# Edge masks of a graph layer made on GpSimd between adjacency products, with a new order of the pair loop

## The chip, the cores and the metric

The kernel runs on one core of a Trainium2 chip. The metric is the device time of one execution in microseconds (us); each figure below is the median of several executions, with the lowest and highest beside it where that matters. The engines are called by the names in the profile: PE (TensorE), PEld (its weight loads), DVE (VectorE), ACT (ScalarE), POOL (GpSimd), SP (SyncE, which issues transfers).

## The reference, cut to what matters

There are 3327 nodes with 64 features and a dense adjacency of fp32 zeros and ones. Layer 0 is a hyperbolic graph layer: for every pair of nodes it needs an attention weight and the logarithmic map of one node at the other, and sums over the neighbours. Layer 1 weights each node's last 100 neighbours by powers of one half, according to their rank from the right.

```python
# layer 0
adj_att = sigmoid(left[:, None] + right[None, :] + b_att[0]) * adj
x_local = logmap(x[:, None, :], x[None, :, :], c)
support_t = einsum('ij,ijd->id', adj_att, x_local)
out0 = proj(expmap(x, support_t, c), c)
# layer 1
mask = (adj != 0).astype(support.dtype)
rank = jnp.cumsum(mask, axis=1)
deg = rank[:, -1:]
k = jnp.minimum(deg, 100.0)
pos = rank - (deg - k)
w = mask * jnp.where(pos > 0, 0.5 ** (k - pos), 0.0)
out1 = w @ support + bias
```

What matters is what the adjacency is read for. Layer 0 multiplies it, as fp32, into the sigmoid. Layer 1 needs a bf16 mask of it, so that PE can count with triangular matrices how many neighbours lie to the right.

## The kernel before

The adjacency is cut into four strips of columns (8, 8, 6 and 4 blocks of 128) and each strip into rounds of at most 1024 columns' worth. A round loads a tile `ad`, makes the mask, lets PE add to the counts in PSUM (`pc`), reads the counts out as uint8 (on ACT or on DVE), builds the sigmoid (a tanh, then the *adjacency product*), computes the pair products in PSUM (`pq`), puts two gelus over them, multiplies with the sigmoid (the *final product*), and lets PE sum (the *total*, in `po`).

```python
for b0, nb in STRIPS:
    ...                                   # loads and left factors of the strip
    for hi in range(NB, 0, -per):
        ad = work.tile([P, FMAX], F32, name="ad", bufs=4)
        nc.sync.dma_start(ad..., adj_t[lo * P : hi * P, i0 : i0 + F]...)
        mask = work.tile([P, FMAX], BF16, name="mask", bufs=3)
        V.tensor_scalar(mask[:, :span], ad[:, :span], 0.0, None, op0=ALU.not_equal)
        for j in js:
            ...                           # counts: matmuls with ca (block before) and cb (this block)
            if j % (2 if b0 == 0 else 4):
                A.activation(kept, pc[:, :F], AF.Relu)
            else:
                V.tensor_scalar(kept, pc[:, :F], 0.0, None, op0=ALU.max)
        sg = work.tile([P, FMAX], F32, name="sg", bufs=3)
        for j in js:
            A.activation(part(sg, j), left_b[:, :F], AF.Tanh, bias=right[:, j : j + 1], scale=0.5)
        V.scalar_tensor_tensor(sg[:, :span], sg[:, :span], 1.0, ad[:, :span], op0=ALU.add, op1=ALU.mult)
        pq = ps.tile([P, FMAX], F32, name="pq", bufs=2)
        ...                               # two matmuls per half and block
        s = work.tile([P, FMAX], F32, name="s", bufs=3)
        A.activation(s[:, :span], pq[:, :span], AF.Gelu, scale=-WG / QS)
        A.activation(s[:, :span], s[:, :span], AF.Gelu, scale=WH)
        V.scalar_tensor_tensor(s[:, :span], s[:, :span], WD, sg[:, :span], op0=ALU.add, op1=ALU.mult)
        ...                               # total of this round into po
        next(steps, None)                 # one step of the post-processing of the strip before
```

The sums of a finished strip are post-processed during the next one, by many short DVE instructions on 128x8 numbers (norms, reciprocal square roots) and some on 128x512, slipped in between the rounds.

Of the kernel before, what the change touches and what calls it, by code (L numbers as in the profile page):

```python
# [11 lines left out]
F32 = mybir.dt.float32  # L12
F16 = mybir.dt.float16
BF16 = mybir.dt.bfloat16
# [3 lines left out]
AF = mybir.ActivationFunctionType  # L18
# [4 lines left out]
P = 128  # L23
# [3 lines left out]
D = 64  # L27
K = D + 2
STRIPS = [(0, 8), (8, 8), (16, 6), (22, 4)]
FMAX = 8 * P  # L30
JH = 13

GSTRIPS = [(0, 7), (7, 7), (14, 6), (20, 6)]
GFMAX = 7 * P
# [30 lines left out]


HS = 1024.0
CNT = 127.0


def halves(n):
    return [(a, min(a + 512, n)) for a in range(0, n, 512)]
# [363 lines left out]
def fast(ctx, tc, x, adj_t, r, w_att, b_att, weight, bias, out, flag):  # L436
# [27 lines left out]
    def column(value, name):  # L464
# [13 lines left out]
    G.memset(ca, -1.0)  # L478
    G.affine_select(out=cb, in_=ca, compare_op=ALU.is_gt, fill=0.0, base=0,
                    pattern=[[-1, P]], channel_multiplier=1)  # L480
    G.affine_select(out=cb, in_=cb, compare_op=ALU.not_equal, fill=CNT, base=0,
                    pattern=[[-1, P]], channel_multiplier=1)
    G.tensor_sub(ca, ca, cb)
    row1 = const.tile([1, P], BF16, name="row1")
    G.memset(row1, 1.0)
    rowc = const.tile([1, 512], BF16, name="rowc")
    G.memset(rowc, MAX_NEIGH - CNT)

    node = const.tile([P, NB], F32, name="node")
    G.memset(node, 1.0)  # L490
# [34 lines left out]
    behind_hi = const.tile([P, NB - JH, NP], U8, name="behind_hi")  # L525
    s2 = const.tile([P, NB, 2, D], F16, name="s2")

    post_pool = ctx.enter_context(tc.tile_pool(name="post", bufs=1))
    pairs = ctx.enter_context(ExitStack())
    ps = pairs.enter_context(tc.tile_pool(name="ps", bufs=1, space=PSUM))  # L530

    with tc.tile_pool(name="pre", bufs=1) as pre:
# [102 lines left out]
        V.tensor_mul(right, plr[:, :, 1], yr)  # L635
        V.tensor_scalar(right, right, batt, 0.5, op0=ALU.add, op1=ALU.mult)


        wn, opx = small("wn"), small("opx")
        V.tensor_scalar(wn, nrm, WA / 2, None, op0=ALU.mult)  # L640
# [16 lines left out]
    def behind(j):  # L657
        return behind_lo[:, j] if j < JH else behind_hi[:, j - JH]

    def in_range():  # L660

        st = post_pool.tile([P, 4], F32, name="st")
        t1 = post_pool.tile([P, NB], F32, name="st1")
        V.tensor_mul(t1, nrm, node)
        V.tensor_reduce(st[:, 0:1], t1, AX.X, ALU.max)
        V.scalar_tensor_tensor(t1, x2, c_c, t1, op0=ALU.mult, op1=ALU.mult)
        V.tensor_reduce(st[:, 1:2], t1, AX.X, ALU.max)
        V.tensor_mul(t1, bal, node)
        V.tensor_reduce(st[:, 2:3], t1, AX.X, ALU.max)
        V.tensor_reduce(st[:, 3:4], t1, AX.X, ALU.min)  # L670
        V.tensor_scalar(st[:, 3:4], st[:, 3:4], -1.0, None, op0=ALU.mult)
        pf = ps.tile([P, P], F32, name="pq", bufs=2)
        T.transpose(pf[:4, :], st, ident)
        st2 = post_pool.tile([4, 1], F32, name="st2")
        V.tensor_reduce(st2, pf[:4, :], AX.X, ALU.max)
        pf = ps.tile([P, P], F32, name="pq", bufs=2)
        T.transpose(pf[:1, :4], st2, ident[:4, :4])
        st3 = post_pool.tile([1, 4], F32, name="st3")
        V.tensor_copy(st3, pf[:1, :4])
        ok = post_pool.tile([1, 2], F32, name="ok")  # L680

        V.tensor_mul(ok, st3[:, 0:4:2], st3[:, 1:4:2])
        V.tensor_scalar(ok[:, 0:1], ok[:, 0:1], QMAX / 2, None, op0=ALU.is_le)
        V.tensor_scalar(ok[:, 1:2], ok[:, 1:2], 0.0, None, op0=ALU.is_equal)
        V.tensor_mul(ok[:, 0:1], ok[:, 0:1], ok[:, 1:2])
        V.tensor_scalar(flag, ok[:, 0:1], -1.0, 1.0, op0=ALU.mult, op1=ALU.add)
# [95 lines left out]
        V.tensor_sub(s2[:, bs, 1], w, s2[:, bs, 0])  # L782


    steps = iter(())
    for b0, nb in STRIPS:
        F = nb * P
        i0 = b0 * P
        hv = halves(F)
        blocks = slice(b0, b0 + nb)  # L790
        queue = nc.scalar if b0 == 0 else nc.sync

        iz = strip.tile([P, 8, P], F16, name="iz")[:, :nb]
        iu = strip.tile([KB, 8, P], F16, name="iu")[:, :nb]
        queue.dma_start(iu[:D], ju[:D, blocks])
        queue.dma_start(iu[D:], ju[KB : KB + 7, blocks])
        queue.dma_start(iz[:D], jz[D:, blocks])
        queue.dma_start(iz[D:], jz[:D, blocks])
        izf, iuf = iz.rearrange("p b q -> p (b q)"), iu.rearrange("p b q -> p (b q)")
        pc = ps.tile([P, FMAX], F32, name="pc")  # L800
        po = ps.tile([P, FMAX], F32, name="po")
        pl = ps.tile([P, FMAX], F32, name="pq", bufs=2)
        for b in range(nb):
            T.transpose(pl[:, b * P : (b + 1) * P], left[:, b0 + b : b0 + b + 1].to_broadcast([P, P]), ident)
        left_b = strip.tile([P, FMAX], F32, name="left_b", bufs=1)
        A.copy(left_b[:, :F], pl[:, :F])
        for f0, f1 in hv:
            T.matmul(pc[:, f0:f1], row1, rowc[:, : f1 - f0], start=True, stop=True, skip_group_check=True)

        per = FMAX // F  # L810
        before = None
        for hi in range(NB, 0, -per):
            lo = max(hi - per, 0)
            js = range(hi - 1, lo - 1, -1)
            span = (hi - lo) * F

            def part(t, j, a=0, b=F):
                return t[:, (j - lo) * F + a : (j - lo) * F + b]

            ad = work.tile([P, FMAX], F32, name="ad", bufs=4)  # L820
            nc.sync.dma_start(ad[:, :span].rearrange("p (b f) -> p b f", f=F),
                              adj_t[lo * P : hi * P, i0 : i0 + F].rearrange("(b p) f -> p b f", p=P))
            mask = work.tile([P, FMAX], BF16, name="mask", bufs=3)
            V.tensor_scalar(mask[:, :span], ad[:, :span], 0.0, None, op0=ALU.not_equal)  # L824
            for j in js:
                now = part(mask, j)
                for f0, f1 in hv:
                    if before is not None:
                        T.matmul(pc[:, f0:f1], ca, before[:, f0:f1], start=False, stop=True, skip_group_check=True)  # L829
                    T.matmul(pc[:, f0:f1], cb, now[:, f0:f1], start=False, stop=True, skip_group_check=True)  # L830
                before = now
                kept = behind(j)[:, i0 : i0 + F]
                if j % (2 if b0 == 0 else 4):
                    A.activation(kept, pc[:, :F], AF.Relu)  # L834
                else:
                    V.tensor_scalar(kept, pc[:, :F], 0.0, None, op0=ALU.max)  # L836


            sg = work.tile([P, FMAX], F32, name="sg", bufs=3)
            for j in js:  # L840
                A.activation(part(sg, j), left_b[:, :F], AF.Tanh, bias=right[:, j : j + 1], scale=0.5)  # L841
            V.scalar_tensor_tensor(sg[:, :span], sg[:, :span], 1.0, ad[:, :span], op0=ALU.add, op1=ALU.mult)  # L842

            pq = ps.tile([P, FMAX], F32, name="pq", bufs=2)
            for j in js:
                for f0, f1 in hv:
                    T.matmul(part(pq, j, f0, f1), ju[:KB, j, :], iuf[:, f0:f1], start=True, stop=False)  # L847
                    T.matmul(part(pq, j, f0, f1), jz[:, j, :], izf[:, f0:f1], start=False, stop=True)  # L848
            s = work.tile([P, FMAX], F32, name="s", bufs=3)
            A.activation(s[:, :span], pq[:, :span], AF.Gelu, scale=-WG / QS)  # L850
            A.activation(s[:, :span], s[:, :span], AF.Gelu, scale=WH)  # L851
            V.scalar_tensor_tensor(s[:, :span], s[:, :span], WD, sg[:, :span], op0=ALU.add, op1=ALU.mult)  # L852
            for j in js:
                for f0, f1 in hv:
                    T.matmul(po[: D + 1, f0:f1], hw[:, j, :], part(s, j, f0, f1), start=j == NB - 1, stop=j == 0)  # L855
                next(steps, None)
        for _ in steps:
            pass

        ot = work.tile([P, FMAX], F32, name="s", bufs=3)[: D + 1]  # L860
        V.tensor_copy(ot[:, :F], po[: D + 1, :F])
        pa = ps.tile([P, FMAX], F32, name="pq", bufs=2)
        for b in range(nb):
            c0 = (b // 4) * 512 + (b % 4) * (D + 1)
            T.transpose(pa[:, c0 : c0 + D + 1], ot[:, b * P : (b + 1) * P], ident[: D + 1, : D + 1])
        agg = post_pool.tile([P, 8, D + 1], F32, name="agg", bufs=2)
        for c in range(0, nb, 4):
            n = min(4, nb - c)
            A.copy(agg[:, c : c + n], pa[:, c * P : c * P + n * (D + 1)].rearrange("p (b d) -> p b d", b=n))
        steps = post(agg[:, :nb], b0, nb)  # L870
        if b0 == 0:
            in_range()
    pairs.close()


# [4 lines left out]
    with tc.tile_pool(name="l1", bufs=2) as l1, tc.tile_pool(name="l1_ps", bufs=1, space=PSUM) as l1_ps:  # L880
# [16 lines left out]
        for j in range(late):  # L897
            wt = decode(j)
            for n in range(len(chunks)):
                add(j, wt, n)  # L900
            for _ in range(2):
                next(steps, None)
        for _ in steps:
            pass
        weights = [decode(j) for j in range(late, NB)]
# [70 lines left out]
```

## Time and profile before

| | before |
|---|---|
| time, us (3 executions) | 460.64 (459.14 to 461.43) |
| profiled span, us | 459.1 |
| pair loop, us (first adjacency product at 47.9 to the last strip's copy at 390.3) | 342.3 |
| DVE busy, us | 407.1 |
| POOL busy, us | 13.3 |

The profile is read in three steps: which engine has no room left, in which stretch of the time, and which instructions fill it. The prediction shows those three views. A group line gives the source line, engine, operation, output and inputs by name and shape, the count, then the busy time and the mean of one in ns, then the idle time just before them and what ended most of it.

### The profile page before, as it was taken

Reading aid. Unit: us, or ns where it says so; the run is one execution under the profiler, and the core shown is the slowest. Engines: PE = TensorE matmul, PEld = TensorE weight load, DVE = VectorE, ACT = ScalarE, POOL = GpSimd, SP = SyncE. Lnnn points to the kernel's source line nnn. Section 1 sums busy time; section 2 is a strip of 40 time slices with the busy share of each in tenths; the row PEclk is TensorE's granted clock in tenths of the full one; section 3 lists DMA queues with packets and bytes.
Section 4 is the critical chain, followed back from the end, with each engine's and each line's share of the span. In section 5 each row is a group of like instructions: output and inputs, shape, how many; then the busy total and the mean of one; then the engine's idle time right before and its main releaser. Section 6 shows DMA issues by size and latency. Waiting matters only on the chain.

```text
span 459.1 us, 4660 instructions
## 1 busy us (share of the span) xinstructions
PE 378.4 (82%) x1484; PEld 153.4 (33%) x1484; DVE 407.1 (89%) x774; ACT 369.2 (80%) x423; POOL 13.3 (3%) x30
## 2 busy tenths in 40 slices
PE   0266699999989799999997999889778897699293
PEld 0035233333323233333333444434322332244152
DVE  3895689999988999999998999999999998999821
ACT  1445989999894999999995999999599995888310
POOL 6000000000000000001000000020000000000000
PEclk9997699999999999999999999999999998899877
DMA  7103354545541444444442444344533420000003
GB/s 201 62 1 72 105 168 143 141 151 163 167 135 46 133 143 140 137 137 137 137 127 75 136 137 140 106 128 125 168 93 111 121 89 1 1 1 1 0 0 82
DMA packets 22840, 47.77 MB, mean 104 GB/s; under 512 B 8652, under 2 KB 9082, under 8 KB 22808
## 3 DMA queue, kind: packets, MB, share of 16 engines
q1 hardware_dynamic: 20522, 46.47, 34.7%
q10 hardware_dynamic: 2062, 0.87, 0.9%
q0 software_dynamic: 224, 0.07, 0.3%
q8 instruction: 13, 0.21, 0.2%
q14 instruction: 19, 0.16, 0.1%
HBM read 45.22 MB, written 0.85 MB: 100 GB/s over the span
## 4 chain that ended last, share of the span: by engine, by line

## 5 line engine op out<-in xcount | busy, mean ns | idle before, releaser
L855 PE MATMUL po<-s,hw 128*65 128x512 f32 (+1 forms) x364 | 165.3, 576 | 11.5 <-DVE s L852 11.1
L842 DVE SCALAR_TENSOR_TENSOR sg<-sg,ad 128x1024 f32<-128x1024 f32 (+1 forms) x91 | 103.5, 1141 | 7.5 <-ACT sg L841 7.3
L852 DVE SCALAR_TENSOR_TENSOR s<-s,sg 128x1024 f32<-128x1024 f32 (+1 forms) x91 | 104.8, 1152 | 3.7 <-ACT s L851 3.6
L841 ACT ACTIVATE sg<-left_b,right 128x1024 f32<-128x1024 f32 (+2 forms) x104 | 102.7, 1001 | 0.1
L851 ACT ACTIVATE s<-s 128x1024 f32<-128x1024 f32 (+1 forms) x91 | 91.4, 1006 | 0.1
L850 ACT ACTIVATE s<-pq 128x1024 f32<-128x1024 f32 (+1 forms) x91 | 87.7, 969 | 2.6 <-PE pq L848 2.6
L829 PE MATMUL pc<-mask,ca 128*128 128x512 bf16 (+1 forms) x175 | 65.7, 375 | 17.3 <-DVE behind_hi L836 7.2
L855 PEld LDWEIGHTS po<-s,hw 128*65 128x65 f32 x364 | 45.2, 138 | 98.9 <-issue 52.7
L847 PE MATMUL pq<-iu,ju 71*128 71x512 f16 (+1 forms) x182 | 67.8, 374 | 11.6 <-ACT s L850 11.6
L830 PE MATMUL pc<-mask,cb 128*128 128x512 bf16 (+1 forms) x182 | 66.7, 376 | 5.3 <-DVE mask L824 5.1
L848 PE MATMUL pq<-iz,jz 128*128 128x512 f16 (+1 forms) x182 | 66.6, 371 | 0.0
L824 DVE TENSOR_SCALAR mask<-ad 128x1024 bf16<-128x1024 f32 (+1 forms) x91 | 59.3, 654 | 3.4 <-PE pc L829 1.8
L894 PE MATMUL pw<-wt,s 128*128 128x512 bf16 (+1 forms) x182 | 41.0, 390 | 12.9 <-DVE s L782 9.2
L834 ACT ACTIVATE behind_hi<-pc 128x1024 uint8<-128x1024 f32 (+2 forms) x37 | 31.8, 860 | 24.3 <-PE pc L830 24.1
L830 PEld LDWEIGHTS <-cb 128*128 128x128 bf16 x182 | 17.9, 99 | 57.8 <-issue 46.6
L834 ACT ACTIVATE behind_lo<-pc 128x1024 uint8<-128x1024 f32 (+2 forms) x33 | 28.2, 853 | 7.1 <-PE pc L830 6.4
L894 PEld LDWEIGHTS <-s 128*128 128x128 f16 x182 | 18.7, 103 | 35.0 <-DVE s L782 9.6
L848 PEld LDWEIGHTS <-jz 128*128 128x128 f16 x182 | 18.1, 99 | 31.5 <-issue 15.3
L829 PEld LDWEIGHTS <-ca 128*128 128x128 bf16 x175 | 17.5, 100 | 30.8 <-issue 19.5
L847 PEld LDWEIGHTS <-ju 71*128 71x128 f16 x182 | 18.1, 100 | 21.4 <-issue 4.8
L836 DVE TENSOR_SCALAR behind_lo<-pc 128x1024 uint8<-128x1024 f32 (+2 forms) x19 | 19.9, 1050 | 1.1 <-PE pc L830 1.1
L771 POOL TENSOR_TENSOR x_sb<-x_sb,bias_b 128x512 f32<-128x512 f32 (+2 forms) x4 | 6.3, 1577 | 418.4 <-DVE w L769 418.4
(209 smaller groups left out, 290.0 us busy)
## 6 DMA issues: line engine op xcount, KB each, us to landing
ad<-in_adj_t SPq DMA_DIRECT2D x65, 512.0 KB, 3.7
ad<-in_adj_t SPq DMA_DIRECT2D x26, 384.0 KB, 3.3
out<-o SPq DMA_DIRECT2D x6, 128.0 KB, 2.0
x_sb<-in_x SPq DMA_DIRECT2D x1, 416.0 KB
x_sb<-in_x ACTq DMA_DIRECT2D x1, 416.0 KB, 6.9
iz<-jz ACTq DMA_DIRECT2D x2, 128.0 KB
iz<-jz SPq DMA_DIRECT2D x2, 128.0 KB, 2.4
iz<-jz SPq DMA_DIRECT2D x2, 96.0 KB
```

What stands on the lines that cost most here:

```text
L829: T.matmul(pc[:, f0:f1], ca, before[:, f0:f1], start=False, stop=True, skip_group_check=True)
L830: T.matmul(pc[:, f0:f1], cb, now[:, f0:f1], start=False, stop=True, skip_group_check=True)
L834: A.activation(kept, pc[:, :F], AF.Relu)
L841: A.activation(part(sg, j), left_b[:, :F], AF.Tanh, bias=right[:, j : j + 1], scale=0.5)
L842: V.scalar_tensor_tensor(sg[:, :span], sg[:, :span], 1.0, ad[:, :span], op0=ALU.add, op1=ALU.mult)
L847: T.matmul(part(pq, j, f0, f1), ju[:KB, j, :], iuf[:, f0:f1], start=True, stop=False)
L848: T.matmul(part(pq, j, f0, f1), jz[:, j, :], izf[:, f0:f1], start=False, stop=True)
L850: A.activation(s[:, :span], pq[:, :span], AF.Gelu, scale=-WG / QS)
L851: A.activation(s[:, :span], s[:, :span], AF.Gelu, scale=WH)
L852: V.scalar_tensor_tensor(s[:, :span], s[:, :span], WD, sg[:, :span], op0=ALU.add, op1=ALU.mult)
L855: T.matmul(po[: D + 1, f0:f1], hw[:, j, :], part(s, j, f0, f1), start=j == NB - 1, stop=j == 0)
L894: T.matmul(pw[n], s2[:, j].rearrange("p c d -> p (c d)"), wt[:, f0:f1].bitcast(BF16), start=j == 0, stop=j == NB - 1)
```

## The change

The mask leaves DVE, the engine that bounds the loop, for GpSimd, which is nearly idle. Because a mask there is slower, it is made three rounds ahead, and it is tied to the end of an adjacency product so that it runs beside DVE instructions with a PSUM input. With the room won, DVE takes over count reads from ACT. Both gelus stay in PSUM, the final product reads PSUM, and each round is emitted as total of the last one, products of the next, count of three ahead, with strip borders bridged. Left factors of later strips come by DMA, the counts need no seeds, and a range check moves to the last layer.

```diff
+AHEAD = 3
+SGB = 4
+ON_ACT = ((1, 6), (2, 5), (1, 2), (1, 2))
...
-            mask = work.tile([P, FMAX], BF16, name="mask", bufs=3)
-            V.tensor_scalar(mask[:, :span], ad[:, :span], 0.0, None, op0=ALU.not_equal)
...
+    def edges(n):
+        mask_of[n] = mask = work.tile([P, FMAX], BF16, name="mask", bufs=3)
+        made = G.tensor_scalar(mask[:, : span(n)], ad_of[n][:, : span(n)], 0.0, 0.0,
+                               op0=ALU.is_equal, op1=ALU.is_equal)
+        if n - AHEAD in sg_inst:
+            tc.add_manual_dep(made.ins, sg_inst[n - AHEAD].ins.name, ...)
...
-            s = work.tile([P, FMAX], F32, name="s", bufs=3)
-            A.activation(s[:, :span], pq[:, :span], AF.Gelu, scale=-WG / QS)
-            A.activation(s[:, :span], s[:, :span], AF.Gelu, scale=WH)
-            V.scalar_tensor_tensor(s[:, :span], s[:, :span], WD, sg[:, :span], op0=ALU.add, op1=ALU.mult)
...
+        for n in range(R):
+            m = n + AHEAD
+            ...                           # load(m + 1), then total(n - 1)
+            A.activation(pq[:, :w], pq[:, :w], AF.Gelu, scale=-WG / QS)
+            A.activation(pq[:, :w], pq[:, :w], AF.Gelu, scale=WH)
+            sg_inst[n] = V.scalar_tensor_tensor(sg[:, :w], sg[:, :w], 1.0, ad_of.pop(n)[:, :w], ...)
+            read(); edges(m); products(n + 1); sigmoids(n + 1)
+            ...                           # steps of the post-processing
+            read(); count(m, ...)
+            V.scalar_tensor_tensor(sg[:, :w], pq[:, :w], WD, sg[:, :w], op0=ALU.add, op1=ALU.mult)
```

The two `is_equal` in the mask mean (ad == 0) == 0, so two compares per element. `ON_ACT` is the share of the count reads of each strip that stays on ACT.

## The prediction

> **What bounds the kernel now.** I began with the busy table of the page, because a kernel with five engines is read by which of them has no room left.
>
> ```profile
> PE 378.4 (82%) x1484; PEld 153.4 (33%) x1484; DVE 407.1 (89%) x774; ACT 369.2 (80%) x423; POOL 13.3 (3%) x30
> ```
>
> VectorE leads, ScalarE and TensorE are close behind, and GpSimd is nearly free. Averages over stages mislead, so next came the busy time in stretches. The five cuts are the four strips of the pair loop (columns of the adjacency: 8, 8, 6 and 4 blocks), found from the copies of the finished sums out of PSUM at 143, 247, 330 and 390 us, and the last layer.
>
> ```profile
> 47.00:143.00 96.00, 89.98 (x289) 31.77 (x288) 87.58 (x88) 87.45 (x90) 0.00 (x0) 0.96 0.49 146
> 143.00:247.00 104.00, 96.34 (x332) 34.26 (x331) 101.53 (x176) 97.18 (x105) 2.19 (x1) 1.00 0.44 129
> 247.00:331.00 84.00, 74.52 (x327) 33.92 (x326) 81.75 (x167) 76.88 (x106) 2.40 (x1) 1.00 0.45 129
> 331.00:391.00 60.00, 50.64 (x164) 17.36 (x163) 56.48 (x127) 52.56 (x78) 1.00 (x1) 0.97 0.27 79
> 391.00:459.00 68.00, 47.18 (x238) 24.91 (x238) 48.06 (x109) 35.83 (x21) 0.73 (x1) 0.85 0.06 14
> ```
>
> The columns are length, then busy time of PE, weight loads, DVE, ACT and POOL, then clock, DMA share and GB/s. The loop takes 344 of 459 us. In it DVE is busy 87.6 + 101.5 + 81.8 + 56.5 = 327.3 us (95%), ACT 314.1 (91%). From strip 1 on DVE is at 94 to 98%. So DVE bounds the loop, with ACT 13 us behind. DMA has room (share under 0.5). What DVE does there is in the costliest groups:
>
> ```profile
> L842 DVE SCALAR_TENSOR_TENSOR sg<-sg,ad 128x1024 f32<-128x1024 f32 (+1 forms) x91 | 103.5, 1141 | 7.5 <-ACT sg L841 7.3
> L852 DVE SCALAR_TENSOR_TENSOR s<-s,sg 128x1024 f32<-128x1024 f32 (+1 forms) x91 | 104.8, 1152 | 3.7 <-ACT s L851 3.6
> L824 DVE TENSOR_SCALAR mask<-ad 128x1024 bf16<-128x1024 f32 (+1 forms) x91 | 59.3, 654 | 3.4 <-PE pc L829 1.8
> L836 DVE TENSOR_SCALAR behind_lo<-pc 128x1024 uint8<-128x1024 f32 (+2 forms) x19 | 19.9, 1050 | 1.1 <-PE pc L830 1.1
> ```
>
> Per round: one adjacency product, one final product, one mask, sometimes a read of the counts out of PSUM. Recorded durations overlap: two such products that follow each other start 1.13 us apart though each lasts 1.22, so in sums I use distances between starts: 1.13 (1024 wide) and 0.87 (768) for a product, 0.61 and 0.47 for a mask, 1.14, 0.87 and about 0.60 (512) for a read. On ACT: tanh 1.04, first gelu 0.90, second gelu 0.95, read 0.90 (0.69 and 0.53 for narrower ones).
>
> **What the Trainium skill says.** First, the two engines that the change couples. "SBUF — State Buffer", section "Who interferes with whom", says that a DVE instruction with two SBUF inputs contends with a GpSimd instruction that reads SBUF, that DVE's two-port modes contend too, and that one with at most one SBUF input outside those modes does not. The trace agrees; in order of time:
>
> ```profile
> 306.80 2.40 POOL L771 TENSOR_TENSOR x_sb<-x_sb,bias_b 128x512 f32<-128x512 f32 x1 [89.06 <-DVE w L769]
> ...
> 308.56 1.45 DVE L852 SCALAR_TENSOR_TENSOR s<-s,sg 128x768 f32<-128x768 f32 x1
> ...
> 381.46 1.00 POOL L771 TENSOR_TENSOR x_sb<-x_sb,bias_b 128x384 f32<-128x384 f32 x1 [72.27 <-DVE w L769]
> ```
>
> The product beside GpSimd's addition took 1.45 us where its like takes 0.95, and the addition 2.40 us where the 384 wide one took 1.00. A contact costs DVE 0.5 us and GpSimd about 1. Second, "GPSIMD Engine Reference", section "4.1 Engine selection", calls one-input operations roughly line-rate and two-input ones about twice as slow as DVE. The additions of 384 (1.00 us) and 256 (0.73) give 2.1 ns per element with two inputs; no long one-input instruction is in this trace. My estimate for the 1024-wide mask is 1.0 us (line rate) to 2.3 us (the two-input slope). Third, "ScalarE: Activation LUTs", section "Step-by-step: what each stage is for", calls PSUM the lower-latency destination for an ACTIVATE. Here the first gelu, which reads PSUM, lasts 1030 ns, and the second, SBUF to SBUF, 1068; no run writes PSUM yet. I count nothing for it.
>
> **The change, part by part.**
>
> *Masks.* 87 of the 91 lie in the loop: 61 x 0.61 + 26 x 0.47 = 49.4 us leave DVE. On GpSimd they take at most 2.3 us of a round of about 3.5, and are wanted three rounds later: hidden. Each is tied to the end of an adjacency product, so that it runs beside the count read (PSUM source) and the final product, which now takes one input from PSUM; both are free of contact.
>
> *Count reads.* The new shares give DVE 21, 15, 13 and 13 reads of 26 per strip instead of 13, 7, 7 and 7: 16 x 1.13 + 6 x 0.87 + 6 x 0.60 = 26.9 us more on DVE, and 16 x 0.90 + 6 x 0.69 + 6 x 0.53 = 21.7 us fewer on ACT. DVE in the loop: 327.3 - 49.4 + 26.9 = 304.8.
>
> *ACT.* Three copies of the left factors go (0.90 + 0.69 + 0.53 = 2.1; a DMA brings them), and one of two table loads (1.28) before the first gelu. Against it: the two gelus are emitted back to back. In the built order 47 pairs now follow each other directly, before 8; such a pair costs 1.05 us between starts (121.78 to 122.83) where 0.90 is usual: 39 x 0.15 = 5.9 us. Sum: 314.1 - 21.7 - 2.1 - 1.3 + 5.9 = 294.9.
>
> *PE.* Nothing but six seeds of the count and 18 of 26 transposes goes. A full round is 16 issue slots of 0.216 us (four matmuls for the count, four for the products, two fp32 ones that take four slots each), 3.46 us, near 3.5 with the weight loads; the loop holds 26 x 26 x 128 / 1024 = 84.5 full rounds: 296 us. The order is now strict: total of the last round, products of the next, count of three ahead.
>
> *Gelus in place.* The two product buffers in PSUM, once free after the first gelu, are now held until the final product on DVE. A buffer's tour is total 1.77, products 0.86, drain 0.2, gelus 1.05 + 1.0, final product 1.2, some 0.3 of waits: 6.4 us for two rounds, 3.2 a round if DVE takes the final product at once. It does not always: each delay beyond 0.3 to 0.4 us shows up as an idle PE.
>
> *Ends.* In the preamble four masks leave DVE (at 13.2, twice after, at 21.2), of which the first three stand before reductions that could start: about 2 us. The strip borders, where ACT idled 4.0 to 4.5 us for the first counts of the next strip, are bridged; DVE hardly idled there, so only about 2 us. The range check moves from the loop into the last layer: 1.5 us each way.
>
> *Sum.* The three engines now need 304.8, 296 and 294.9. Before, the loop lasted 344 for a bound of 327.3, so 17 us were lost to start-up and handoffs. Bridged borders give back 2. Contact costs: in 14 places DVE's order has two adjacency products in a row, so a mask meets one: 14 x about 0.3 on average = 4. Three nearly equal engines with tighter buffers: 4 more, by judgement. Loop: 305 + 17 - 2 + 4 + 4 = 328, 16 saved. With 2 from the preamble: 460.6 - 18 = 442.6, say 442.
>
> **Rivals.** (a) *The product buffers bind.* With PSUM held through DVE, PE, ACT and DVE wait in a ring. For: 3.2 a round plus one full wait of 1.13 for DVE is over 3.7, what strip 0 takes now (96 / 26); DVE's order in the later strips is irregular, with post-processing between. Against: ACT still has 10% of room. The loop would save 0 to 6 us, giving 453 to 460. (b) *GpSimd is slow or in the way.* If a mask takes 2.3 us and meets an adjacency product each time there is no count read, DVE loses about 29 x 0.5 = 15 us, giving 455; if it took over 3.5 us GpSimd would bound the loop at 84.5 x 3.5 or more, and nothing is gained. Against: a 128 x 128 one-input cast on GpSimd starts 0.25 us before the next instruction, fixed cost included, under 2.0 ns per element. (c) *The schedule is as good as meant.* Counts are never waited for, the 17 us shrink to 7, and the loop is PE's and DVE's at 312: 426. For: PE's order is perfectly regular in strips 0 to 2. Against: balance of three engines seldom runs at 97%.
>
> **Range and chances.** I take 442 with a range of 429 (most of c) to 455 (the mild end of a or b). Faster by 2% means below 451.4; that leaves 9 us under my estimate for a and b, so 0.79. Within 2%: 0.18. Slower would need both rivals at once: 0.03.
>
> **What would show it.** Right: masks of 1.0 to 2.3 us on GpSimd with POOL busy 100 to 200 us; DVE busy near 385 in all and still first or level with PE; adjacency products at 1.22 us on average, not 1.5; strips 0 to 3 near 93, 98, 79 and 56 us; ACT without waits for counts at strip borders. Wrong: long waits of PE's totals and products for the final product and of the first gelu for its products (a); adjacency products stretched, or matmuls of the count waiting for masks (b).

## The result and the profile after

The changed kernel took **482.72 us** (481.46 to 484.36, 4 executions) against 461.03 (459.14 to 463.85, 4 executions) of the kernel before in the same rounds: a ratio of 1.0467 with a 95% interval of 1.04 to 1.0534. It is slower, and 28 us above the top of the predicted range. Here and below, a ratio is the mean time of one kernel's fast runs over that of the other's of the same rounds, so it is not quite the ratio of the medians quoted.

The busy line of the page after:

```profile
PE 375.9 (78%) x1443; PEld 154.3 (32%) x1460; DVE 409.8 (85%) x712; ACT 351.8 (73%) x391; POOL 332.3 (69%) x119
```

POOL went from 13 to 332 us, where I had named 100 to 200. DVE did not fall to 385: it is busier than before (409.8 us against 407.1), with 62 instructions fewer. The stretches, cut at the same events as before (first adjacency product, the four copies of finished sums, end); the columns are as in the prediction:

```profile
48.09:147.27 99.18, 93.13 (x303) 34.00 (x309) 87.56 (x75) 86.35 (x86) 97.58 (x27) 0.95 0.51 150
147.27:260.97 113.70, 97.81 (x314) 35.34 (x317) 101.60 (x150) 89.20 (x96) 100.32 (x28) 0.94 0.39 117
260.97:350.91 89.94, 73.83 (x318) 33.41 (x318) 84.31 (x151) 74.39 (x101) 79.91 (x27) 1.00 0.43 125
350.91:412.71 61.80, 48.02 (x144) 16.18 (x144) 53.75 (x104) 45.53 (x65) 36.30 (x11) 0.94 0.18 52
412.71:482.60 69.89, 46.36 (x236) 24.81 (x240) 50.73 (x130) 36.05 (x21) 0.72 (x1) 0.87 0.06 14
```

All four strips grew: 99, 114, 90 and 62 us against 95, 104, 83 and 60 before. In strip 0 POOL is busy for 97.6 of 99.2 us. In strips 1 to 3 no engine is full: DVE is at 89, 94 and 87%. The groups, in the order of the page:

```profile
L857 POOL TENSOR_SCALAR mask<-ad 128x1024 bf16<-128x1024 f32 (+1 forms) x91 | 321.5, 3554 | 64.0 <-DVE sg L965 33.5
...
L895 ACT ACTIVATE sg<-left_b,right 128x1024 f32<-128x1024 f32 (+2 forms) x104 | 101.8, 982 | 36.0 <-PE po L912 35.0
L987 DVE SCALAR_TENSOR_TENSOR sg<-pq,sg 128x1024 f32<-128x1024 f32 (+1 forms) x91 | 103.6, 1138 | 18.0 <-ACT pq L963 17.5
L965 DVE SCALAR_TENSOR_TENSOR sg<-sg,ad 128x1024 f32<-128x1024 f32 (+1 forms) x91 | 107.9, 1186 | 8.8 <-ACT sg L895 8.7
L874 PE MATMUL pc<-mask,cb 128*128 128x512 bf16 (+1 forms) x179 | 65.8, 378 | 47.9 <-POOL mask L857 47.2
...
L888 DVE TENSOR_SCALAR behind_hi<-pc 128x1024 uint8<-128x1024 f32 (+2 forms) x29 | 30.6, 1054 | 11.1 <-PE pc L874 11.1
```

A mask takes 3.55 us on average, not 1.0 to 2.3. PE's count matmuls wait 47.2 us for masks. The adjacency products are hardly longer (1186 ns against 1141), so most of DVE's extra busy time is not in them. The tanh, early in its round, waits 35.0 us for totals of PE; my reading is that the scheduler lets it run ahead until its four `sg` buffers are full, and then a late PE holds it.

The length of a mask that nothing disturbs is read from the timeline, whose columns are start, length, engine, instruction. The entry below merges the 27 masks made in strip 0, which follow each other without a gap. Taken one by one, 26 of them last 3.62 or 3.63 us and one 4.38; most starts are 3.59 us apart, since recorded durations overlap a little.

```profile
49.57 97.99 POOL L857 TENSOR_SCALAR mask<-ad 128x1024 bf16<-128x1024 f32 x27 [29.22 <-DVE sg L965]
```

And a piece of strip 1 shows where DVE's extra time went:

```profile
199.84 1.21 DVE L965 SCALAR_TENSOR_TENSOR sg<-sg,ad 128x1024 f32<-128x1024 f32 x1
199.93 4.62 POOL L857 TENSOR_SCALAR mask<-ad 128x1024 bf16<-128x1024 f32 x1
...
200.98 0.99 DVE L743 TENSOR_TENSOR y<-u,k 128x8 f32<-128x8 f32 x1
...
201.90 0.15 DVE L745 TENSOR_TENSOR xy<-xy,k 128x8 f32<-128x8 f32 x1
```

L743 and L745 are two like instructions of the post-processing, with two SBUF inputs of eight numbers per partition each, both issued while the mask runs. The first takes 0.99 us, the second 0.15. The adjacency product, which started before the mask, shows the other direction: the mask took 4.62 us where an undisturbed one takes 3.62, so it got going about 1.00 us late, at 200.93. The first short instruction was 0.84 us late, at 201.82. So it was let go some 0.9 us after the mask had got going, and the mask ran on until 204.55 without holding the second one.

This distance is no accident. Of the 52 DVE instructions that are over 0.1 us longer than their like in e7 (below, without masks), 44 were let go, by the same working, 0.87 to 0.91 us after a mask of 1024 columns got going, or 0.67 to 0.69 us after one of 768. So a mask of 3.62 us held DVE only in its first 0.9 us; why it did so is not shown.

This gave the theory for the experiments. **Contact**: the masks hold up DVE's short post-processing instructions, of which the prediction had thought only as fillers. **Pace**: a mask of 3.62 us is longer than a round of PE (3.45 us, the distance of the totals in an undisturbed stretch), so GpSimd falls behind, uses up the lead of three, and PE waits. Late in strip 0 the totals do come 3.58 to 3.61 us apart, which is the masks' own distance. **Rivals**: that the new order, the shares or the PSUM buffers cost the time by themselves, or that too few `sg` buffers do.

### The profile page after: what moved, and what is told of

It reads as the page before. It is cut to its first block, busy times and chain, and to the rows that moved or that the text cites. A ratio compares the mean times of both kernels' runs of the same rounds, so it can differ in the third digit from the quotient of the medians.

```text
span 482.6 us, 4843 instructions
## 1 busy us (share of the span) xinstructions
PE 375.9 (78%) x1443; PEld 154.3 (32%) x1460; DVE 409.8 (85%) x712; ACT 351.8 (73%) x391; POOL 332.3 (69%) x119
## 4 chain that ended last, share of the span: by engine, by line
PE 32%; DVE 32%; POOL 14%; ACT 10%; issue 9%; DMA 2%; POOLq 0%; DVEq 0%; ACTq 0%
PE po L912 13%; POOL mask L857 13%; DVE sg L987 7%; DVE sg L965 6%; PE pw L1014 5%; PE pc L874 4%; PE pq L902 3%; PE pq L903 3%; PE pc L873 2%; ACT pq L963 2%; ACT sg L895 2%; DVE behind_lo L888 2%; ACT pq L962 2%; DVE wt L1009 2%; DMA w<-in_weight 2%
## 5 line engine op out<-in xcount | busy, mean ns | idle before, releaser
L857 POOL TENSOR_SCALAR mask<-ad 128x1024 bf16<-128x1024 f32 (+1 forms) x91 | 321.5, 3554 | 64.0 <-DVE sg L965 33.5
L912 PE MATMUL po<-sg,hw 128*65 128x512 f32 (+1 forms) x364 | 170.6, 592 | 14.3 <-DVE sg L987 13.2
L987 DVE SCALAR_TENSOR_TENSOR sg<-pq,sg 128x1024 f32<-128x1024 f32 (+1 forms) x91 | 103.6, 1138 | 18.0 <-ACT pq L963 17.5
L965 DVE SCALAR_TENSOR_TENSOR sg<-sg,ad 128x1024 f32<-128x1024 f32 (+1 forms) x91 | 107.9, 1186 | 8.8 <-ACT sg L895 8.7
L874 PE MATMUL pc<-mask,cb 128*128 128x512 bf16 (+1 forms) x179 | 65.8, 378 | 47.9 <-POOL mask L857 47.2
L962 ACT ACTIVATE pq<-pq 128x1024 f32<-128x1024 f32 (+1 forms) x91 | 86.1, 946 | 8.4 <-PE pq L903 8.3
L963 ACT ACTIVATE pq<-pq 128x1024 f32<-128x1024 f32 (+1 forms) x91 | 86.6, 951 | 1.5
L912 PEld LDWEIGHTS po<-sg,hw 128*65 128x65 f32 x364 | 48.5, 142 | 97.8 <-issue 60.7
L873 PE MATMUL pc<-mask,ca 128*128 128x512 bf16 (+1 forms) x165 | 61.6, 373 | 12.5 <-DVE behind_hi L888 6.8
L888 DVE TENSOR_SCALAR behind_hi<-pc 128x1024 uint8<-128x1024 f32 (+2 forms) x29 | 30.6, 1054 | 11.1 <-PE pc L874 11.1
L888 DVE TENSOR_SCALAR behind_lo<-pc 128x1024 uint8<-128x1024 f32 (+2 forms) x33 | 34.4, 1043 | 2.1 <-PE pc L874 1.9
L881 ACT ACTIVATE behind_hi<-pc 128x1024 uint8<-128x1024 f32 (+2 forms) x23 | 18.9, 821 | 12.0 <-PE pc L874 11.9
```

The lines of the kernel that those rows point to most:

```text
L857: made = G.tensor_scalar(mask[:, : span(n)], ad_of[n][:, : span(n)], 0.0, 0.0, op0=ALU.is_equal, op1=ALU.is_equal)
L873: T.matmul(S.pc[:, f0:f1], ca, S.before[:, f0:f1], start=False, stop=True, skip_group_check=True)
L874: T.matmul(S.pc[:, f0:f1], cb, now[:, f0:f1], start=S.first, stop=True, skip_group_check=True)
L912: T.matmul(S.po[: D + 1, f0:f1], hw[:, j, :], part(n, s_of[n], j, f0, f1), start=j == NB - 1, stop=j == 0)
L962: A.activation(pq[:, :w], pq[:, :w], AF.Gelu, scale=-WG / QS)
L963: A.activation(pq[:, :w], pq[:, :w], AF.Gelu, scale=WH)
```

## The experiments

Twelve kernels ran; all gave correct results. They ran in three groups on three chips; the kernel before took 460.52 us in the first (e1 to e4), 461.44 in the second (e5 to e8) and 459.30 in the third (e9 to e12), 7 executions each, and 4 of each experiment. So a difference between kernels of different groups is uncertain by some 2 us. Unless said otherwise the edit is to the changed kernel.

### e1_cast and e2_one_op: a shorter mask on GpSimd

```diff
-        made = G.tensor_scalar(mask[:, : span(n)], ad_of[n][:, : span(n)], 0.0, 0.0,
-                               op0=ALU.is_equal, op1=ALU.is_equal)
+        made = G.tensor_copy(mask[:, : span(n)], ad_of[n][:, : span(n)])          # e1
+        made = G.tensor_scalar(mask[:, : span(n)], ad_of[n][:, : span(n)], 0.0, None, op0=ALU.is_gt)   # e2
```

Both are right for an adjacency of zeros and ones. Expected of e1:

> The mask is made on GpSimd by a plain cast of the adjacency (0 and 1 here, so the result stays right) in place of the two compares; nothing else differs from the changed kernel. Theory P (pace): GpSimd needs 3.63 us for a 1024-wide mask where TensorE can do a round in 3.45, so it sets the pace and eats the lead. If the cast takes 1.0 to 2.3 us, the counts no longer wait for masks (47 us before), the rounds return to about 3.5 us, and the time falls to 435 to 455. Theory O (order): the scheduler let the tanh run ahead until it stands before a total of the round before (35 us of ScalarE waiting), and the product buffers are held in PSUM; then a faster mask changes little: 470 to 483.

Expected of e2:

> The mask on GpSimd by one compare (greater than zero) in place of two. It measures what an operation of the pair costs. Theory P: the time follows the duration of the mask; if one compare halves it to about 1.8 us the time is that of the cast within 5 us; if the duration stays at 3.6 us because it is a cost per element of the instruction and not of its operations, 478 to 486. Theory O: 470 to 483 whatever the mask takes.

Measured: e1 468.93 us (468.59 to 469.67), ratio 1.0174 (1.0134 to 1.0215); e2 471.16 (470.96 to 472.05), ratio 1.0216 (1.0176 to 1.0255). The 1024-wide masks, by form, in the changed kernel, e1 and e2:

```profile
L857 POOL TENSOR_SCALAR mask<-ad 128x1024 bf16<-128x1024 f32 x65 | 246.0, 3807 | 53.0 <-DVE sg L965 32.6 <-PE pq L903 6.3 <-DVE sa L717 3.2
```

```profile
L857 POOL CAST mask<-ad 128x1024 bf16<-128x1024 f32 x65 | 85.3, 1315 | 193.5 <-DVE sg L964 72.7 <-PE pc L872 44.2 <-PE pq L902 17.4
```

```profile
L857 POOL TENSOR_SCALAR mask<-ad 128x1024 bf16<-128x1024 f32 x65 | 202.9, 3135 | 80.1 <-DVE sg L964 46.4 <-PE pq L902 6.0 <-PE pc L873 3.9
```

Means of 3.81, 1.32 and 3.14 us (undisturbed 3.62, 1.04 and 2.76) give 482.7, 468.9 and 471.2 us. Cutting a mask from 3.1 to 1.3 us is worth 2 us, from 3.8 to 3.1 it is worth 12. So the cost of length sets in somewhere between 3.1 and 3.8 us; PE's round of 3.45 us lies in between, as pace says, but three points place it no closer. Yet the cast, at a third of a round, still leaves a kernel slower than before. Its busy line shows why it is not pace that remains:

```profile
PE 373.9 (80%) x1443; PEld 150.7 (32%) x1460; DVE 413.1 (88%) x712; ACT 351.4 (75%) x391; POOL 122.3 (26%) x119
```

DVE is as busy as with the slow masks: a cast of 1.04 us holds it as long as two compares of 3.62. All 50 DVE instructions of e1 that are over 0.1 us longer than in e7 were let go 0.87 to 0.91 us (1024 columns) or 0.67 to 0.69 us (768) after a cast got going. Here long instructions are met too. The adjacency products take 115.0 us, against 103.7 in e7, because twelve of them in strip 0 last 2.04 to 2.11 us; their group, and one of the twelve:

```profile
L964 DVE SCALAR_TENSOR_TENSOR sg<-sg,ad 128x1024 f32<-128x1024 f32 (+1 forms) x91 | 115.0, 1265 | 5.6 <-ACT sg L894 5.6
```

```profile
75.57 1.04 POOL L857 CAST mask<-ad 128x1024 bf16<-128x1024 f32 x1 [3.19 <-PE pc L872]
...
75.64 2.05 DVE L964 SCALAR_TENSOR_TENSOR sg<-sg,ad 128x1024 f32<-128x1024 f32 x1
```

The tie did not keep this cast off the product: by the trace it had waited 3.19 us for a count of PE, and it started 0.07 us before the next adjacency product.

Three waits of PE for a mask are left, 18.6 us. The longest, 12.5 us, lies before the loop, at the very start (the changed kernel has one of 12.7 there among its 47.2), so the loop has 6.1 us of them, against 34.5 in the changed kernel.

### e3_vector_mask: everything but the masks

```diff
-ON_ACT = ((1, 6), (2, 5), (1, 2), (1, 2))
+ON_ACT = ((1, 2), (3, 4), (3, 4), (3, 4))
...
-        made = G.tensor_scalar(..., 0.0, 0.0, op0=ALU.is_equal, op1=ALU.is_equal)
+        made = V.tensor_scalar(..., 0.0, None, op0=ALU.not_equal)
-        if n - AHEAD in sg_inst: ...      # the tie
```

> The changed kernel with the masks back on VectorE and the shares of count reads as before (half, then three of four on ScalarE), so that only the rest of the change is left: gelus in place, rounds emitted with a lead of three, left factors by DMA. Theory P: VectorE is loaded as before (327 us of the loop), so 450 to 466. Theory O: the new order itself costs; 472 to 490.

Measured: 457.22 us (456.63 to 458.68), ratio 0.9926 (0.9884 to 0.9967). The new order, gelus in place and bridged borders with the masks on DVE are harmless, and worth some 0.7%. So the loss is the masks' move, not the order or the PSUM buffers. The shares of count reads are the old ones here; e7 clears the new ones.

### e4_sg6: more buffers for the tanh

```diff
-SGB = 4
+SGB = 6
-        ad_of[n] = ad = work.tile([P, FMAX], F32, name="ad", bufs=AHEAD + 3)
+        ad_of[n] = ad = work.tile([P, FMAX], F32, name="ad", bufs=AHEAD + 2)
```

One `ad` buffer goes to make room in SBUF.

> Six buffers for the tanh tiles in place of four (and one adjacency buffer fewer to make room); masks stay on GpSimd. Theory P: the pace is GpSimd's, so ScalarE's waits for totals only move elsewhere: 477 to 486. Theory O: the 35 us that ScalarE waited for totals go, and a good part of them shows: 445 to 470.

Measured: 474.71 us (472.42 to 475.11), ratio 1.028 (1.0232 to 1.0329): 8 us better than the changed kernel, still slower than before. ACT's wait for totals fell from 35.0 to 20.6 us. The buffers took part in the loss; e9 tells whether as a cause or as a follower.

### e5_idle_casts and e6_idle_fills: contact alone

Both start from e3, where DVE makes the masks and nothing waits for GpSimd, and add one GpSimd instruction a round whose result nobody reads, tied as in the change. The cast reads and writes SBUF, the fill only writes. The rule in e6's expectation is the one that the prediction takes from the Trainium skill, "SBUF — State Buffer", section "Who interferes with whom".

```diff
+        V.tensor_scalar(mask[:, : span(n)], ad_of[n][:, : span(n)], 0.0, None, op0=ALU.not_equal)
+        idle = work.tile([P, FMAX], BF16, name="idle", bufs=2)
+        made = G.tensor_copy(idle[:, : span(n)], ad_of[n][:, : span(n)])    # e5
+        made = G.memset(idle[:, : span(n)], 1.0)                            # e6
```

> The kernel with the masks on VectorE and the old shares (457.2 us) plus one cast of the adjacency tile on GpSimd in each round, tied to the adjacency product as the masks were, into a tile that nothing reads. Nothing waits for it, so all that it can cost is contact: VectorE instructions with two SBUF inputs held while GpSimd reads SBUF. Theory C (contact): the trace of the cast run has VectorE busy some 30 us more than its work explains, mostly in the short post-processing instructions; here the same, so 472 to 490. Theory P (pace) alone: 455 to 461.

> The same kernel, but GpSimd fills the idle tile with a constant in place of casting the adjacency: it writes SBUF and reads nothing. Theory C with the skill's rule that only GpSimd's reads meet VectorE's second input: no cost, 455 to 461. If its writes or its mere activity were the cost: 465 to 490, near the run with the idle casts.

Measured: e5 474.72 us (473.05 to 477.05), ratio 1.0303 (1.0256 to 1.035); e6 458.68 (458.34 to 459.44), ratio 0.9954 (0.9923 to 0.9985). Against e3 the casts cost 17.5 us and the fills 1.5, which is within the spread between the groups of runs; against the fills, which ran in the same group, the casts cost 16.0. The busy lines of e3, e5 and e6:

```profile
PE 369.3 (81%) x1437; PEld 149.7 (33%) x1460; DVE 403.2 (89%) x772; ACT 370.3 (81%) x422; POOL 10.6 (2%) x28
```

```profile
PE 377.5 (79%) x1460; PEld 151.5 (32%) x1460; DVE 424.1 (89%) x772; ACT 372.4 (78%) x422; POOL 116.8 (25%) x119
```

```profile
PE 370.7 (81%) x1460; PEld 149.8 (33%) x1460; DVE 406.2 (89%) x772; ACT 370.7 (81%) x422; POOL 106.5 (23%) x119
```

POOL is busy for nearly as long in e6 as in e5, but only the reading instruction stretches DVE, by 20.9 us against 3.0. One group of the post-processing, of e5 and then e6, shows the same:

```profile
L510 DVE SCALAR_TENSOR_TENSOR rn<-rs_t,rn 128x8 f32<-128x8 f32 (+2 forms) x36 | 8.1, 226 | 0.3
```

```profile
L510 DVE SCALAR_TENSOR_TENSOR rn<-rs_t,rn 128x8 f32<-128x8 f32 (+2 forms) x36 | 5.6, 157 | 0.3
```

The mean of 226 ns mixes 32 instructions of about 0.16 us with four of 0.58 to 1.00. Contact is shown, without any wait for a mask. The granted clock of TensorE does not explain the difference: at 0.967 an execution of e5 took 473.05 us, at 0.965 one of e6 458.34; and at 0.950 one of the changed kernel took 481.46, one of e7 444.74.

### e7_no_mask: no mask at all

A 1.0 in fp32 has a 1.0 in bf16 as its upper half, and 0.0 has 0.0. So PE can count directly from every second bf16 of the adjacency tile.

```diff
-        mask_of[n] = mask = work.tile([P, FMAX], BF16, name="mask", bufs=3)
-        made = G.tensor_scalar(...)
-        if n - AHEAD in sg_inst: ...      # the tie
+        mask_of[n] = ad_of[n].bitcast(BF16).rearrange("p (f c) -> p f c", c=2)[:, :, 1]
```

This is right for any adjacency of zeros and ones, which the inputs are, and wrong for other weights.

> No masks at all: the count reads the upper halves of the fp32 adjacency (1.0 in fp32 ends in the bf16 1.0) as a strided bf16 tile, right only for an adjacency of 0 and 1 as here. Everything else, the new shares and the order, is the changed kernel's. It is the changed kernel with masks that cost nothing on any engine: 49 us off VectorE and no GpSimd. Theory C and P together: the rest of the prediction holds, 432 to 450. Theory O (the order and the held product buffers cost): 455 or more. If TensorE reads a stride of two slower (the counts' matmuls further apart than 0.216 us), that shows in the trace.

Measured: **444.18 us** (442.29 to 444.74), ratio 0.963 (0.9595 to 0.9664). It beats both kernels, and it is the world of the prediction, with masks that cost nothing. Its busy line, its four strips, and its adjacency products:

```profile
PE 373.2 (84%) x1460; PEld 151.4 (34%) x1460; DVE 383.0 (87%) x712; ACT 349.4 (79%) x391; POOL 10.6 (2%) x28
```

```profile
50.29:144.65 94.36, 91.21 (x294) 32.73 (x295) 81.22 (x71) 84.84 (x85) 0.00 (x0) 0.96 0.52 158
144.65:239.96 95.31, 93.21 (x321) 33.45 (x320) 93.35 (x150) 89.49 (x98) 1.26 (x1) 1.00 0.46 139
239.96:319.26 79.30, 74.00 (x319) 32.98 (x318) 75.90 (x151) 73.74 (x101) 1.27 (x1) 1.00 0.49 141
319.26:371.74 52.48, 46.64 (x146) 15.70 (x144) 49.05 (x103) 44.95 (x65) 1.00 (x1) 0.97 0.21 61
```

```profile
L958 DVE SCALAR_TENSOR_TENSOR sg<-sg,ad 128x1024 f32<-128x1024 f32 (+1 forms) x91 | 103.7, 1140 | 6.5 <-ACT sg L888 6.3
```

DVE executes the same 712 instructions as in the changed kernel, in 383.0 instead of 409.8 us, with the new shares of count reads. Group by group, adjacency products make 4.2 us of the 26.8; final products and count reads differ by 0.1 us a group; the rest sits in the post-processing and a few instructions of the preamble. Every second bf16 as the moving operand costs PE little: count matmuls start 0.22 to 0.23 us apart (0.226 on average), against 0.215 with the contiguous mask of the changed kernel.

```profile
99.86 0.39 PE L866 MATMUL pc<-ad,ca 128*128 128x512 bf16 x1
100.08 0.39 PE L867 MATMUL pc<-ad,cb 128*128 128x512 bf16 x1
100.31 0.39 PE L866 MATMUL pc<-ad,ca 128*128 128x512 bf16 x1
```

### e8_before_pool_mask: the masks alone, in the old kernel

To the kernel before, with the shares of the change:

```diff
-            V.tensor_scalar(mask[:, :span], ad[:, :span], 0.0, None, op0=ALU.not_equal)
+            G.tensor_scalar(mask[:, :span], ad[:, :span], 0.0, 0.0, op0=ALU.is_equal, op1=ALU.is_equal)
...
-                if j % (2 if b0 == 0 else 4):
+                if (NB - 1 - j) % (6 if b0 == 0 else 5 if b0 == 8 else 2) < (2 if b0 == 8 else 1):
```

> The kernel before with two parts of the change alone: the masks on GpSimd by the two compares, and the new shares of count reads. Its order, its three buffers and its gelus in SBUF stay. Theory P and C: as slow as the changed kernel or slower, 475 to 500, since each mask is made only as far ahead as the scheduler puts it, and nothing keeps it off the adjacency products. Theory O: faster than the changed kernel, 455 to 470.

Measured: 491.5 us (488.79 to 493.41), ratio 1.0659 (1.0608 to 1.0711); DVE busy 426.9. The masks do their damage in the old order too, and more of it: the rest of the change wins back 9 us, and no run says which part of it. One part shows in the groups: with its inputs in SBUF the final product is held too, and takes 112.9 us here, where it takes 104.8 in the kernel before and 103.6 in the changed one, which reads PSUM.

### e9_no_mask_sg6: buffers without masks

e7 with `SGB = 6` as in e4; the `ad` buffers stay at six.

> The kernel without masks (444.2 us) with six tanh tiles in place of four. With four, ScalarE waited 12.8 us in it for totals. With masks on GpSimd six of them gave 8 us (482.7 to 474.7). If the buffers cost by themselves: 436 to 442. If the tanh tiles mattered only because late masks held everything up: 442 to 446.

Measured: 445.23 us (444.58 to 445.32), ratio 0.9672 (0.9614 to 0.973), the same as e7. Four `sg` buffers are enough when counts are on time. Where the counts are on time, more of them gain nothing; what e4 gained with them hangs on late masks.

### e10_cast_no_tie: the tie

e1 without the tie of the mask to the adjacency product.

```diff
-        if n - AHEAD in sg_inst:
-            tc.add_manual_dep(made.ins, sg_inst[n - AHEAD].ins.name, ...)
```

> The kernel with the mask as a cast on GpSimd (468.9 us), without the tie of each mask to the end of an adjacency product. Theory C: the tie is meant to keep the masks off the adjacency products, but VectorE's order has other two-input instructions in between; without it more of the products are met, or the casts run early while VectorE is elsewhere. If the tie protects: 474 to 490. If it does nothing, since contact is with the post-processing anyway: 465 to 473. If it does harm, by starting every mask just when the next product comes: 450 to 465.

Measured: 471.48 us (470.1 to 472.78), ratio 1.0244 (1.0178 to 1.031), DVE busy 414.6 against 413.1. The tie is worth 2 or 3 us at most; the intervals of the two ratios overlap, so it may be worth nothing. With it and without it masks meet adjacency products, which take 115.0 us in e1 and 113.4 in e10, and the post-processing.

### e11_vector_mask_sg6: a better balance with the mask on DVE

```diff
-SGB = 4
-ON_ACT = ((1, 6), (2, 5), (1, 2), (1, 2))
+SGB = 6
+ON_ACT = ((2, 3), (5, 6), (5, 6), (5, 6))
...                                        # mask on DVE and no tie as in e3, one ad buffer fewer as in e4
```

> An attempt at a version that beats both and stays right for any adjacency: masks on VectorE with the new order (457.2 us), six tanh tiles, and still more count reads on ScalarE (two of three in strip 0, five of six after). That moves 9 to 10 reads, some 10 us, from VectorE to ScalarE, which has 81% to VectorE's 89%. If VectorE sets the pace: 446 to 454. If ScalarE becomes the bound: 456 to 464.

Measured: 463.77 us (462.11 to 465.18), ratio 1.0086 (1.0018 to 1.0154). The attempt failed: the time lies in the range that was named for ScalarE as the bound.

```profile
PE 373.2 (81%) x1460; PEld 152.3 (33%) x1460; DVE 394.4 (86%) x761; ACT 378.6 (82%) x433; POOL 11.0 (2%) x28
```

DVE lost 9 us of work against e3 and the kernel became 7 us slower. The work given to ACT, 378.6 against 370.3 us, may be what it now waits on (DVE waits 17.0 us for second gelus), but the share, the buffers and the schedule changed together, and no run separates them. It stays open.

### e12_before_no_mask: no masks, in the old kernel

To the kernel before, with the shares of the change and six `ad` buffers, since counts now hold them:

```diff
-            mask = work.tile([P, FMAX], BF16, name="mask", bufs=3)
-            V.tensor_scalar(mask[:, :span], ad[:, :span], 0.0, None, op0=ALU.not_equal)
+            mask = ad.bitcast(BF16).rearrange("p (f c) -> p f c", c=2)[:, :, 1]
-            ad = work.tile([P, FMAX], F32, name="ad", bufs=4)
+            ad = work.tile([P, FMAX], F32, name="ad", bufs=6)
...                                        # shares as in e8
```

> The kernel before without masks (the count reads the upper halves of the fp32 adjacency; six adjacency buffers), with the new shares of count reads, but its own order, its gelus in SBUF and its strip borders. Beside the run without masks in the new order (444.2 us) it tells what order, lead and gelus in place are worth once the masks are free. If they are worth what they gave with masks on VectorE, 3 us: 445 to 450. If they are worth more when VectorE is not the only bound: 450 to 458. If the held product buffers cost: 430 to 442.

Measured: 446.25 us (444.98 to 447.62), ratio 0.9691 (0.9627 to 0.9755). The old kernel gets nearly all of e7's gain from three small edits: no mask, more `ad` buffers, new shares. The new order, lead, gelus in place and bridged borders together are worth 2 us between e12 and e7, and the intervals overlap. So the gain comes from the masks' time leaving DVE, with the reads redistributed into it; how the two share it was not tested.

## Why the prediction was wrong

**The sum without the masks' cost.** The prediction said 442, and e7, where the masks cost nothing, took 444.2. DVE busy "near 385" was 383.0. ACT in the loop was worked out as 294.9; the four stretches of e7 give 84.84 + 89.49 + 73.74 + 44.95 = 293.0. The strips were named near 93, 98, 79 and 56 us and took 94, 95, 79 and 52. Two smaller terms were off and cancelled: the loop saved 20.8 us (342.3 to 321.5) where 16 were foreseen, while the preamble and the last layer, where 2 were to be saved, lost 4.2 in e7 (first adjacency product at 50.29 instead of 47.94; 70.8 us after the last strip instead of 68.9). Why they lost was not followed up. (A slip without weight: seven seeds of the count go, not six.)

**The step that failed first: "At most 2.3 us of a round of about 3.5 ... hidden".** It took 3.62 us undisturbed, longer than the round, and 91 masks kept POOL busy for 321.5 us. The upper estimate came from additions with two inputs, the lower one from the skill's line rate for one input, and neither does what the instruction does. The cast of e1, undisturbed at 1.04 us, fell on the lower estimate; one compare takes 2.76 us, two take 3.62. In these three the cost hangs on the operation, since all have one input. The page is silent on that: the Trainium skill, "GPSIMD Engine Reference", section "4.1 Engine selection", says "1-input is roughly line-rate", which holds for e1's cast and not for the compares. What this pace costs is the difference of the changed kernel and e2 or e1: 482.7 - 471.2 = 11.5, or 482.7 - 468.9 = 13.8 us. It is clean to a few us only, since DVE's busy time is not the same in the three (409.8, 406.6 and 413.1 us).

**The step that cost most: "14 x about 0.3 on average = 4".** The size was met by luck: adjacency products lost 4.2 us, and 14 of them were held, but ten of these lie in strip 0, held for 0.12 to 0.66 us, and only two follow another adjacency product. With casts they lost 11.3 us. "Both are free of contact", said of count reads and final products, holds too: their groups are as in e7 to 0.1 us. What the step left out is the other 22.6 of DVE's 26.8 us: the post-processing, and about 2 us in the preamble. The prediction quoted the rule from "SBUF — State Buffer", section "Who interferes with whom", and then applied it only to the long instructions that fill the table of groups; but the rule is about inputs, not length, and a short instruction can lose far more than its own length. In the timeline a 0.15 us instruction took 0.99. What is left of the loss with fast masks is e1 - e7 = 24.7 us, of which at most 6.1 can be the waits for masks left in e1's loop. Where no mask is waited for, e5 lost 16.0 us against e6 and 17.5 against e3. The two ways need not agree, since e5's DVE also makes the masks, so contact costs some 16 to 25 us.

**The sum, corrected.** 444.2 (e7) + 24.7 (mostly contact) + 13.8 (mostly pace) = 482.7. It adds up by the way the terms were taken, as differences of runs; what tests them is e5, e6 and e2. The second and third terms, predicted as 4 and 0, are 38.5 us.

**The rivals.** Rival (a), product buffers that bind, fell: e7 has them in place as the change does, and runs at the predicted time. Rival (b), "GpSimd is slow or in the way", came true in both halves at once: I had priced the slow half as "nothing is gained" and the contact half as 15 us, and did not add them. The argument against it was a 128 x 128 cast, which says nothing about a compare. The 0.03 for "slower" rested on "both rivals at once"; one rival with two parts was enough. Of rival (c), a nearly full PE did come about in e7 (busy for 97, 98 and 93% of strips 0 to 2), but its clean 426 did not.

**Gelus in PSUM.** I had counted nothing. The second gelu of 1024 went from 1068 ns (SBUF to SBUF) to 1012, the first from 1030 (PSUM to SBUF) to 1007. The Trainium skill's remark on PSUM as the lower-latency destination ("ScalarE: Activation LUTs", section "Step-by-step: what each stage is for") agrees, with 23 ns where only the destination changed. What this is worth to the time no run isolates; with order, lead and bridged borders it is within the 2 us between e12 and e7.

## What to carry to other kernels

Before moving work to an idle engine, measure the very instruction there (operation, width and types), and compare its length with the round it has to fit in, not with the idle time on average. When it is GpSimd that will read SBUF, list all DVE instructions with two SBUF inputs that will run meanwhile, the shortest first: each can lose several times its own length. A faster GpSimd instruction need not ease this: here a cast of 1.04 us held DVE as long as a mask of 3.62, 0.9 us each. And ask whether the work is needed at all: reading the upper halves of the numbers already loaded was worth 3.7%, while the best place for the mask was worth less than 1%.

## What the Trainium skill lacked or had wrong

- "GPSIMD Engine Reference", section "4.1 Engine selection": its "1-input is roughly line-rate" is right for a cast (fp32 to bf16, 128x1024: 1.04 us undisturbed) but not for a one-input tensor_scalar with compares: 2.76 us undisturbed with one compare, 3.62 us with two. No page gives the duration of a GpSimd tensor_scalar.
- "SBUF — State Buffer", section "Who interferes with whom": the rule of who meets whom held (casts that read, 17.5 us and 20.9 us of DVE busy time; fills that only write, 1.5 and 3.0). The lock for the whole instruction, which the page's section "SBUF: two separate sides" states for two SBUF inputs as well, did not: a mask that ran until 204.55 us held an instruction of 0.15 us for 0.84 us and let it end at 201.97, and masks of 3.62 us and casts of 1.04 us both held DVE for their first 0.9 us. Some one-input tensor_scalar of the post-processing were held too (a group of 12 took 3.6 us instead of e7's 1.9). At least one was held by itself and not behind a held neighbour: it took 1.00 us at 336.21 in the changed kernel, right after an adjacency product of the usual 0.94. The page allows that for its two-port modes; that this instruction ran in one is not shown.
